# The second transposed m of a Newton iteration, moved from TensorE to a trip through DRAM

## The chip, the cores and the metric

The kernel runs on one NeuronCore of a Trainium2 chip. What counts is the device time of one execution in microseconds (us). Beside it there is a profile of one execution: every instruction of every engine with its start and duration, the packets of the DMA engines, and the semaphores. The engines are called PE (TensorE), DVE (VectorE), ACT (ScalarE), POOL (GpSimd) and SP (SyncE, which here only issues DMAs).

## What is computed

The input x has the shape 32 x 32 x 128 x 128 (images, channels, rows, columns). Two layers follow each other. The first adds to x the matrix square root of a normalised x, by five Newton-Schulz steps on every one of the 1024 matrices of 128 x 128. The second is a spectral layer (Fourier transform, 64 x 32 modes multiplied by weights, inverse transform). The change lies in the first.

```python
A2 = A.reshape(b_s * c, n_c, n_c)
normA = jnp.sqrt(jnp.sum(A2 * A2, axis=(1, 2)))
Y = A2 / normA[:, None, None]
Z = I
for _ in range(5):
    T = 0.5 * (3.0 * I - jnp.matmul(Z, Y))
    Y = jnp.matmul(Y, T)
    Z = jnp.matmul(T, Z)
sA = Y * jnp.sqrt(normA)[:, None, None]

x = x + _L0_conv_ref(_gn(x))
x = x + _L1_conv_ref(_gn(x), L1_conv_weights1, L1_conv_weights2)
```

## The kernel before

The kernel does not run the five steps literally. It works with m, a scaled form of the matrix, and with polynomials of m: two steps at a time are one factor q of degree four, so that the five steps become a first q, a second q, and a last factor t.

**The unit of work** is a set: four channels of one image, held as a tile of 128 x 512 numbers in single precision. There are 256 sets. `products` (L304) multiplies four pairs of 128 x 128 matrices on TensorE into one PSUM bank; `taken` (L271) copies a bank to SBUF on ACT with a factor; `plus` (L279) does bank times factor plus a tile on DVE; `plus_eye` (L290) adds a multiple of the unit matrix on POOL.

TensorE computes the transpose of its left operand times the right one, so a product with m on the left needs m transposed as the left operand. Hence each set carries m and mb, its transposed copy with another scale. Transposes appear in two ways:

- `transposed` (L310) is four TensorE transposes into a bank.
- In `quartic` (L364), the sets called far are turned by way of DRAM: DVE transposes the 32 x 32 blocks (L373), SP writes the result to a DRAM tile (L375), and after some rounds SP reads it back with the blocks in their new places (L383 or L386). POOL then adds r (L388). Sets that are not far use `transposed` and DVE instead. The second `quartic` of a set uses the form called wide, which reads back with four DMAs of 32 partitions each; the first uses one DMA for all 128.

**`newton`** (L400) is the whole course of one set: q from m, mb and r; y from q and m; m from q and y; mb by transposing the new m on TensorE; r from mb; the second q; then two products with that q, the last factor t, and the final product, which DVE adds to xt. It is a generator. Each `yield from rest` gives up the turn twice, and `newton` of a far set gives it up 27 times.

**The order of the work** comes from the loop at the end of the kernel (L997). It has nine lanes, each with one set under way. One pass over all lanes is a round: every lane advances its set by one turn, and between lanes the loop steps other generators: `staged` (normalising the next set, L333), `prep` (statistics of the next image, L187), `settle` and `forward` (what follows a finished set, L426 and L443), `spectrum`, and the products and inverse transforms of the second layer. New sets start at most every FAR = 27/9 = 3 rounds for far sets and every NEAR = 25/5 rounds for others, of which at most about five are under way. A set is far when its image is 1 to 18 (`is_far`, L316, FIRST = 19). So 18 x 8 = 144 sets are far; while they run, little of the second layer's later work is there. I call this time the first stage. The scheduler of the language places instructions by this order and by its own estimate of when they can run; those wrapped in `kept`, all DMAs among them, stay in program order.

**DMA queues.** SP issues writes and reads of the turn buffer, the store of xt to `mid`, and the second layer's transfers. ACT issues the loads b, xt and xs, between its other work.

**Buffers.** `rooms` (L259) gives two numbers for each kind of tile: buffers that exist throughout, and more that exist only until the first stage is over (`four`, L263).

Of the kernel before, what the change touches and what calls it, by code (L numbers as in the profile page):

```python
# [29 lines left out]
F32 = mybir.dt.float32  # L30
AF = mybir.ActivationFunctionType
ALU = mybir.AluOpType
# [4 lines left out]
P = 128  # L37
# [8 lines left out]
QA = 3 + 12 ** (1 / 3)  # L46
QR = 2 * QA - 9
QD = 39 / QA
EYE = 36 / 16
QS = EYE / QD  # L50
MS = -QA * QS
# [17 lines left out]
def conv_preact_kernel(  # L69
# [8 lines left out]
    nc = tc.nc  # L78

    const = ctx.enter_context(tc.tile_pool(name="const", bufs=1))  # L80
    dram = ctx.enter_context(tc.tile_pool(name="dram", bufs=1, space=DRAM))
# [65 lines left out]
    def bank():  # L147
        return ps8.tile([P, 4, P], F32, tag="ps", name="ps")
# [36 lines left out]
    kept = tc.keep_in_program_order  # L185

    def prep(b, made):  # L187
# [12 lines left out]
        for i in range(C // 4):  # L200
# [37 lines left out]
        nc.vector.tensor_scalar_mul(  # L238
            nn, n.rearrange("p g c -> p (g c)"), P * (1.5 / EYE) ** 2
        )  # L240
# [17 lines left out]

    rooms = dict(b=(4, 2), xt=(10, 4), x=(3, 2), r=(5, 2), v=(3, 3), w=(3, 2), q=(4, 2), y=(4, 2))  # L259
    rooms.update(m=(4, 2), mb=(2, 1), t=(3, 2), y4=(2, 2), turn=(0, 4))  # L260
    turns = dict.fromkeys(rooms, 0)

    def four(tag, more):  # L263
        n, m = rooms[tag]
        if more:
            turns[tag] += 1
            if turns[tag] % (n + m) >= n:
                return early.tile([P, 4, P], F32, tag=tag + "_early", name=tag, bufs=m)
        return sets.tile([P, 4, P], F32, tag=tag, name=tag, bufs=n)

    def taken(ps, tag, more, f=1.0):  # L271
        t = four(tag, more)
        if f == 1.0:
            nc.scalar.copy(t, ps)
        else:
            nc.scalar.mul(t, ps, f)  # L276
        return t

    def plus(ps, f, t, tag, more):  # L279

        s = four(tag, more)
        nc.vector.scalar_tensor_tensor(s, ps, f, t, ALU.mult, ALU.add)  # L282
        return s

    def blocks(t):


        return t.rearrange("p c x -> p (c x)").rearrange("p (a c j) -> p a c j", a=4, c=4)

    def plus_eye(mb, far, more):  # L290

        r = four("r", more)
        if far:
            nc.gpsimd.tensor_tensor(
                blocks(r).rearrange("p a c j -> p c a j"),
                mb.rearrange("p c (a j) -> p c a j", a=4),
                eye.rearrange("p c (a j) -> p c a j", a=4),
                ALU.add,
            )
        else:  # L300
            nc.gpsimd.tensor_tensor(r, mb, eye, ALU.add)  # L301
        return r

    def products(lhsT, rhs):  # L304
        ps = bank()
        for j in range(4):
            nc.tensor.matmul(ps[:, j, :], lhsT[:, j], rhs[:, j], start=True, stop=True)  # L307
        return ps

    def transposed(t):  # L310
        ps = bank()
        for j in range(4):
            nc.tensor.transpose(ps[:, j, :], t[:, j, :], ident)
        return ps

    def is_far(b):  # L316
        return 0 < b < FIRST
# [43 lines left out]
        ready.append((xt, m, mb, plus_eye(mb, is_far(b), has_more(b, g))))  # L361
        yield

    def quartic(m, mb, r, far, more, wide):  # L364


        v = plus(products(mb, m), -1 / (QA * QR * QS), m, "v", more)
        if far:


            t = four("turn", more)
            form = "p c (b i) -> p b c i" if wide else "p c (i b) -> p b c i"
            nc.vector.transpose(blocks(t), v.rearrange(form, b=4))  # L373
            held = dram.tile([P, 512], F32, name="turn", tag="turn", bufs=8)
            kept(nc.sync.dma_start(out=held, in_=t.rearrange("p c x -> p (c x)")))  # L375
            yield from rest
            w = four("w", more)
            wb = blocks(w).rearrange("p a c j -> p a (c j)")
            if wide:
                for b in range(4):  # L380
                    rows = slice(32 * b, 32 * b + 32)
                    src = held[:, P * b : P * b + P].rearrange("(a i) x -> i a x", a=4)
                    kept(nc.sync.dma_start(out=wb[rows], in_=src))  # L383
            else:
                src = held.rearrange("(a i) (b x) -> (i b) a x", a=4, b=4)
                kept(nc.sync.dma_start(out=wb, in_=src))  # L386
            yield from rest
            nc.gpsimd.tensor_tensor(w, w, r, ALU.add)  # L388
            w = blocks(w).rearrange("p a c j -> p c a j")
        else:  # L390
            yield from rest
            w = plus(transposed(v), 1.0, r, "w", more)
        yield from rest
        q = plus(products(v, w), 1 / (16 * QS * QS), eye, "q", more)
        yield from rest
        return q

    rest = (None, None)

    def newton(g, sn, xt, m, mb, r, far, more):  # L400


        q = yield from quartic(m, mb, r, far, more, False)
        y = taken(products(q, m), "y", more, 1 / MS)
        yield from rest
        m = taken(products(q, y), "m", more, MS)
        yield from rest
        mb = taken(transposed(m), "mb", more, QR * QS / MS)
        r = plus_eye(mb, far, more)
        yield from rest  # L410
        q = yield from quartic(m, mb, r, far, more, True)
        pw, py = products(q, m), products(q, y)
        w, y = taken(pw, "t", more, 1 / MS), four("y4", more)
        for j in range(4):
            c = 4 * g + j
            nc.scalar.mul(y[:, j, :], py[:, j, :], sn[:, c : c + 1])  # L416
        yield from rest
        t = plus(products(w, q), -0.5 * EYE / 1.5, eye, "t", more)
        yield from rest
        nc.vector.tensor_tensor(xt, products(t, y), xt, ALU.add)  # L420
        yield
# [575 lines left out]
    while todo or any(lanes) or posts or specs or prods or backs:  # L997
# [3 lines left out]
        for i in range(LANES):  # L1001
            step(norms)
            step(loads)
            far = todo and is_far(todo[0][0])
            under_way = [is_far(lane[0]) for lane in lanes if lane]
            room = far or under_way.count(False) + 0.6 * under_way.count(True) < LESS
            if lanes[i] is None and todo and room and rounds >= due:
                due = max(due, rounds - 1) + (FAR if far else NEAR)
                while norms:
                    step(norms)  # L1010
                b, g = todo.pop(0)
                xt = ready[0][0]
# [87 lines left out]
```

## Time and profile before

| What | us |
|---|---|
| median of three runs | 3109.61 |
| lowest and highest run | 3102.69, 3109.81 |
| the profiled execution, its own time | 3100.66 |
| span of the profile, first to last instruction | 3098.6 |
| PE busy in the span | 2948.7 (95%) |
| DVE busy | 2340.0 (76%) |
| POOL busy | 1998.0 (64%) |
| ACT busy | 1704.0 (55%) |
| DMA, mean over the span | 206 GB/s |

The far sets' adds on POOL (L388) start from 108.4 to 1611.8 us, which marks the first stage. Shares over the whole span mix it with the second layer, so the stage has to be read by itself. A product in single precision is two TensorE instructions, a transpose is one; a count of matmuls has to be read with that in mind. Durations of single matmuls overlap, so their price is taken from start to start.

### The profile page before, as it was taken

Reading aid. Unit: us, or ns where it says so; the run is one execution under the profiler, and the core shown is the slowest. Engines: PE = TensorE matmul, PEld = TensorE weight load, DVE = VectorE, ACT = ScalarE, POOL = GpSimd, SP = SyncE. Lnnn points to the kernel's source line nnn. Section 1 sums busy time; section 2 is a strip of 40 time slices with the busy share of each in tenths; the row PEclk is TensorE's granted clock in tenths of the full one; section 3 lists DMA queues with packets and bytes.
Section 4 is the critical chain, followed back from the end, with each engine's and each line's share of the span. In section 5 each row is a group of like instructions: output and inputs, shape, how many; then the busy total and the mean of one; then the engine's idle time right before and its main releaser. Section 6 shows DMA issues by size and latency. Waiting matters only on the chain. (4 is left out here: it accounts for less than half of the span.)

```text
span 3098.6 us, 79471 instructions
## 1 busy us (share of the span) xinstructions
PE 2948.7 (95%) x29760; PEld 2828.6 (91%) x29760; DVE 2340.0 (76%) x5178; ACT 1704.0 (55%) x4153; POOL 1998.0 (64%) x2312
## 2 busy tenths in 40 slices
PE   6999999999999999999999999999999998999994
PEld 6899999999999999999999998998899988899983
DVE  6788887888888787788877555788778766878654
ACT  3566556666665665666654444555454544555552
POOL 3567677677776666677665434768677764777453
PEclk9999999999999999999999999999999999999996
DMA  4576676666666666676743466667676876766666
GB/s 130 164 216 207 202 217 211 210 213 214 212 209 208 209 207 183 201 212 208 219 146 100 143 217 214 226 228 235 206 250 209 269 233 211 236 208 204 194 218 221
DMA packets 475150, 636.78 MB, mean 206 GB/s; under 512 B 97040, under 2 KB 255248, under 8 KB 474768
## 3 DMA queue, kind: packets, MB, share of 16 engines
q1 hardware_dynamic: 361872, 425.88, 42.8%
q10 hardware_dynamic: 112896, 205.83, 21.7%
q8 instruction: 237, 3.88, 0.5%
q14 instruction: 145, 1.19, 0.1%
HBM read 402.42 MB, written 229.11 MB: 204 GB/s over the span
## 5 line engine op out<-in xcount | busy, mean ns | idle before, releaser
L388 POOL TENSOR_TENSOR w<-w,r 128x512 f32<-128x512 f32 x288 | 366.3, 1276 | 324.3 <-DMA w<-turn 274.8
L307 PE MATMUL ps<-w,v 128*128 128x128 f32 x4096 | 554.6, 279 | 18.0 <-DVE w L282 7.7
L341 ACT ACTIVATE b<-b,a_off,a_scr 128x128 f32<-128x128 f32 x1024 | 468.7, 490 | 154.6 <-issue 48.1
L307 PE MATMUL ps<-y,q 128*128 128x128 f32 x4096 | 527.0, 277 | 6.2 <-ACT d L893 2.1
L307 PEld LDWEIGHTS ps<-w,v 128*128 128x128 f32 x4096 | 504.0, 194 | 25.1 <-POOL w L388 11.0
L307 PEld LDWEIGHTS ps<-y,q 128*128 128x128 f32 x4096 | 490.5, 193 | 9.6 <-issue 2.6
L433 POOL TENSOR_TENSOR fold<-xt 128x256 f32<-128x256 f32 x512 | 363.8, 731 | 204.5 <-DVE xt L420 192.2
L282 DVE SCALAR_TENSOR_TENSOR q<-ps,eye 128x512 f32<-128x512 f32 x512 | 348.0, 680 | 156.8 <-PE ps L307 151.5
L827 POOL TENSOR_TENSOR yt<-yt,d 128x512 f32<-128x512 f32 x248 | 311.2, 1282 | 153.7 <-ACT d L893 116.0
L301 POOL TENSOR_TENSOR r<-mb,eye 128x512 f32<-128x512 f32 x112 | 142.7, 1274 | 311.3 <-ACT mb L276 298.8
L348 POOL TENSOR_SCALAR x<-xt,a_nm,a_sc 128x128 f32<-128x128 f32 x736 | 322.7, 451 | 19.5 <-DVE a_n L231 19.5
L416 ACT ACTIVATE y<-ps,a_t_s 128x128 f32<-128x128 f32 x1024 | 291.4, 367 | 58.1 <-PE ps L307 57.6
L202 DVE BATCH_NORM_STATS2 a_st<-xs 128x6 f32<-128x128 f32 x1024 | 229.2, 278 | 108.7 <-DMA xs<-in_xt 107.9
L307 PE MATMUL ps<-m,q 128*128 128x128 f32 x2048 | 276.4, 278 | 8.1 <-DVE q L282 5.2
L307 PE MATMUL ps<-x,b 128*128 128x128 f32 x2048 | 277.0, 279 | 6.8 <-POOL x L348 5.6
L307 PE MATMUL ps<-m,mb 128*128 128x128 f32 x2048 | 276.7, 279 | 6.6 <-ACT d L893 4.3
L307 PE MATMUL ps<-x,q 128*128 128x128 f32 x2048 | 277.8, 279 | 3.3 <-DVE q L282 1.6
L307 PE MATMUL ps<-y,t 128*128 128x128 f32 x2048 | 275.1, 277 | 2.1 <-DVE t L282 2.0
L276 ACT ACTIVATE t<-ps 128x512 f32<-128x512 f32 x256 | 152.3, 595 | 223.1 <-PE ps L307 214.4
L307 PE MATMUL ps<-q,t 128*128 128x128 f32 x2048 | 274.9, 278 | 0.0
L373 DVE STREAM_TRANSPOSE turn<-v 128x512 f32<-128x512 f32 x288 | 262.0, 910 | 4.6
L307 PEld LDWEIGHTS ps<-m,q 128*128 128x128 f32 x2048 | 251.6, 193 | 10.7 <-DVE q L282 5.8
(148 smaller groups left out, 5768.2 us busy)
## 6 DMA issues: line engine op xcount, KB each, us to landing
turn<-turn SPq DMA_DIRECT2D x288, 256.0 KB
b<-in_x ACTq DMA_DIRECT2D x256, 256.0 KB
xt<-in_xt ACTq DMA_DIRECT2D x256, 256.0 KB
xs<-in_xt ACTq DMA_DIRECT2D x256, 256.0 KB
mid<-xt SPq DMA_DIRECT2D x256, 256.0 KB
yt<-mid SPq DMA_DIRECT2D x128, 512.0 KB
out<-yt SPq DMA_DIRECT2D x120, 512.0 KB
w<-turn SPq DMA_DIRECT2D x144, 256.0 KB
```

What stands on the lines that cost most here:

```text
L202: nc.vector.bn_stats(st[:, 4 * i + c, :], tiles[i][:, c, :])
L276: nc.scalar.mul(t, ps, f)
L282: nc.vector.scalar_tensor_tensor(s, ps, f, t, ALU.mult, ALU.add)
L301: nc.gpsimd.tensor_tensor(r, mb, eye, ALU.add)
L307: nc.tensor.matmul(ps[:, j, :], lhsT[:, j], rhs[:, j], start=True, stop=True)
L341: nc.scalar.activation(t, x, AF.Identity, bias=offset[:, c], scale=scale[:, c])
L348: nc.gpsimd.tensor_scalar(m[:, j, :], xt[:, j, :], nm[:, c // 2 : c // 2 + 1], sc[:, c : c + 1], ALU.add, ALU.mult,)
L373: nc.vector.transpose(blocks(t), v.rearrange(form, b=4))
L388: nc.gpsimd.tensor_tensor(w, w, r, ALU.add)
L416: nc.scalar.mul(y[:, j, :], py[:, j, :], sn[:, c : c + 1])
L433: nc.gpsimd.tensor_tensor(f[:, :, 64 * half : 64 * half + 64], xt[:, :, 0:64], xt[:, :, 64:128], op)
L827: engine.tensor_tensor(yh, yh, d, op)
```

## The change

For far sets (`TURNED = 1` takes every one of them), the transposed copy of the second m is made in the way in which v was: block transposes on DVE, a write to DRAM, and reads back. The code of that way becomes a function, `turned`, which always uses the wide form with its four reads. The first `quartic` uses it too. Because mt comes back as m transposed itself, and not as its scaled copy in a bank, the second factor is built the other way round: `quartic` takes m as left and mt as right operand, and mt as what is added. As mt is seen in blocks, the DVE operation for that v is written as four instructions of 128 x 128. In place of the two products of q with m and y, the set computes q times mt, then q times that to form t, then q times t, scaled by ACT, and at last that with y. r is now made from a second copy of the bank that holds m. The buffers change with it: mt gets five, the turn buffer five instead of four, twelve DRAM tiles instead of eight, two more each for y (eight in all), one more each for r and v; b loses one and m two. FAR stays at 27/9, while a far set now gives up its turn 29 times.

```diff
+    rooms.update(mt=(0, 5), turn=(0, 5), b=(4, 1), m=(4, 0), y=(4, 4), r=(5, 3), v=(3, 4), w=(3, 2))
...
-    def quartic(m, mb, r, far, more, wide):
-        v = plus(products(mb, m), -1 / (QA * QR * QS), m, "v", more)
+    def turned(v, tag, more):
+        t = four("turn", more)
+        nc.vector.transpose(blocks(t), v.rearrange("p c (b i) -> p b c i", b=4))
+        held = dram.tile([P, 512], F32, name="turn", tag="turn", bufs=12)
+        kept(nc.sync.dma_start(out=held, in_=t.rearrange("p c x -> p (c x)")))
+        yield from rest
+        w = four(tag, more)
+        wb = blocks(w).rearrange("p a c j -> p a (c j)")
+        for b in range(4):
+            rows = slice(32 * b, 32 * b + 32)
+            src = held[:, P * b : P * b + P].rearrange("(a i) x -> i a x", a=4)
+            kept(nc.sync.dma_start(out=wb[rows], in_=src))
+        yield from rest
+        return w
+
+    def quartic(left, right, f, add, r, far, more):
+        ps = products(left, right)
+        v = four("v", more)
+        whole = len(add.shape) == 3
+        for c in [slice(0, 4)] if whole else range(4):
+            nc.vector.scalar_tensor_tensor(
+                v[:, c] if whole else v[:, c].rearrange("p (a j) -> p a j", a=4),
+                ps[:, c] if whole else ps[:, c].rearrange("p (a j) -> p a j", a=4), f, add[:, c], ALU.mult, ALU.add
+            )
         if far:
...
+            w = yield from turned(v, "w", more)
             nc.gpsimd.tensor_tensor(w, w, r, ALU.add)
...
+    def scaled(ps, g, sn, tag, more):
+        y = four(tag, more)
+        for j in range(4):
+            c = 4 * g + j
+            nc.scalar.mul(y[:, j, :], ps[:, j, :], sn[:, c : c + 1])
+        return y
...
-        m = taken(products(q, y), "m", more, MS)
-        yield from rest
-        mb = taken(transposed(m), "mb", more, QR * QS / MS)
-        r = plus_eye(mb, far, more)
-        yield from rest
-        q = yield from quartic(m, mb, r, far, more, True)
-        pw, py = products(q, m), products(q, y)
-        w, y = taken(pw, "t", more, 1 / MS), four("y4", more)
...
+        pm = products(q, y)
+        m = taken(pm, "m", more, MS)
+        if far and g % TURNED == 0:
+            r = plus_eye(taken(pm, "mb", more, QR * QS), far, more)
+            mt = yield from turned(m, "mt", more)
+            mt = blocks(mt).rearrange("p a c j -> p c a j")
+            q = yield from quartic(m, mt, 1 / (QA * QA * QS), mt, r, far, more)
+            w = taken(products(q, mt), "t", more, 1 / MS)
+            yield from rest
+            t = plus(products(q, w), -0.5 * EYE / 1.5, eye, "t", more)
+            yield from rest
+            t = scaled(products(q, t), g, sn, "y4", more)
+        else:
```

After this, all sets end as before with the product of t and y, which DVE adds to xt. Sets that are not far keep the old course in the branch `else`.

More of the change, by code (lines that the diff above doesn't have):

```diff
@@ L48 @@
 QD = 39 / QA
+TURNED = 1
 EYE = 36 / 16
@@ L362, in staged @@
         yield
-    def quartic(m, mb, r, far, more, wide):
-        v = plus(products(mb, m), -1 / (QA * QR * QS), m, "v", more)
-        if far:
[L371 to L375, printed above, removed]
-            yield from rest
[L377 to L386, printed above, removed]
-            yield from rest
+    def turned(v, tag, more):
[21 more added lines that the diff above has]
+            )
+        if far:
+            w = yield from turned(v, "w", more)
             nc.gpsimd.tensor_tensor(w, w, r, ALU.add)
@@ L398, in conv_preact_kernel @@
     rest = (None, None)
+    def scaled(ps, g, sn, tag, more):
[4 more added lines that the diff above has]
+        return y
     def newton(g, sn, xt, m, mb, r, far, more):
-        q = yield from quartic(m, mb, r, far, more, False)
+        fm = -1 / (QA * QR * QS)
+        q = yield from quartic(mb, m, fm, m, r, far, more)
         y = taken(products(q, m), "y", more, 1 / MS)
         yield from rest
-        m = taken(products(q, y), "m", more, MS)
-        yield from rest
-        mb = taken(transposed(m), "mb", more, QR * QS / MS)
-        r = plus_eye(mb, far, more)
-        yield from rest
-        q = yield from quartic(m, mb, r, far, more, True)
-        pw, py = products(q, m), products(q, y)
-        w, y = taken(pw, "t", more, 1 / MS), four("y4", more)
[L414 to L418, printed above, removed]
+        pm = products(q, y)
[11 more added lines that the diff above has]
+        else:
+            yield from rest
+            mb = taken(transposed(m), "mb", more, QR * QS / MS)
+            r = plus_eye(mb, far, more)
+            yield from rest
+            q = yield from quartic(mb, m, fm, m, r, far, more)
+            pw, py = products(q, m), products(q, y)
+            w = taken(pw, "t", more, 1 / MS)
+            y = scaled(py, g, sn, "y4", more)
+            yield from rest
+            t = plus(products(w, q), -0.5 * EYE / 1.5, eye, "t", more)
         yield from rest
```

## The prediction

> **What bounds the kernel now.** I first asked for the busy time of every engine in a stretch of the first stage (300 to 1300 us), where the change acts.
>
> ```profile
> core 0: us, PE busy (x) PEld busy (x) DVE busy (x) ACT busy (x) POOL busy (x), PEclk, DMA share, GB/s
> 300.00:1300.00 1000.00, 986.59 (x8862) 958.14 (x8861) 818.98 (x1831) 605.12 (x1497) 698.20 (x772) 0.99 0.68 207
> ```
>
> The groups of this stretch count 193 block transposes, two a set, so 96.5 sets pass in 1000 us: 10.36 us a set. TensorE is the bound: busy 98.7% at a granted clock of 0.99, and in the groups by shape hardly any matmul idles before it starts. The reader should note what stands second and third: DVE 82%, the 16 DMA engines 68%. The timeline of TensorE then gives the price of what is removed.
>
> ```profile
> 604.65 0.63 PE L313 MATMUL ps<-ident,z 128*128 128x128 f32 x4
> 605.12 0.60 PE L313 MATMUL ps<-ident,m 128*128 128x128 f32 x4
> 605.56 1.06 PE L307 MATMUL ps<-w,v 128*128 128x128 f32 x8
> 606.45 0.72 PE L307 MATMUL ps<-x,b 128*128 128x128 f32 x5
> ```
>
> Start to start, four transposes take 605.56 - 605.12 = 0.44 us, and the eight matmuls of one product of four 606.45 - 605.56 = 0.89 us. Third, the DVE timeline: the two block transposes of a set are not alike.
>
> ```profile
> 610.62 1.13 DVE L373 STREAM_TRANSPOSE turn<-v 128x512 f32<-128x512 f32 x1
> 611.65 0.68 DVE L420 TENSOR_TENSOR xt<-ps,xt 128x512 f32<-128x512 f32 x1
> ...
> 614.35 0.71 DVE L373 STREAM_TRANSPOSE turn<-v 128x512 f32<-128x512 f32 x1
> ```
>
> The one after the first v (form "i b", strided by four elements) takes 1.13, that of the second (form "b i") 0.71. Fourth, the DMA view and the timeline of SP's queue.
>
> ```profile
> q1 hardware_dynamic: 173189, 130.02, 41.7%
> q10 hardware_dynamic: 41502, 75.56, 25.3%
> ...
> turn<-turn SPq DMA_DIRECT2D x193, 256.0 KB
> ...
> w<-turn SPq DMA_DIRECT2D x97, 256.0 KB
> w<-turn SPq DMA_DIRECT2D x387, 64.0 KB
> ...
> 630.21 0.32 SPq L375 DMA_DIRECT2D turn<-turn  x1
> 631.03 1.77 SPq L383 DMA_DIRECT2D w<-turn  x4
> ```
>
> SP's q1 takes 41.7% of the engines, ACT's q10 25.3%. A "b i" turn is one write and four reads of 64 KB, which hold SP 1.77 us; an "i b" turn needs one read. Last, the waits.
>
> ```profile
> POOL w L388 <- DMA w<-turn: 196.2, 77, 8.3
> ACT mb L276 <- DMA w<-turn: 4.6, 2, 2.4
> SPq L375 <- DMA w<-turn: 16.3, 12, 3.7
> ```
>
> POOL waits for turned tiles in 77 of 193 cases: the round trip through DRAM is already only just in time. The other two name DMAs whose data the waiter does not read. The trace's semaphores explain them: all 2749 DMAs that SP and ACT issue share eight completion semaphores in turn, so the ninth waits until the first has landed, and ACT's evacuations stand behind ACT's issues.
>
> **What the skill says.** The Trainium skill, "DMA: Bandwidth & Descriptors", section "Issuing engines are not separate DMA queues": SP's and ACT's DMAs interleave on the same 16 engines. The trace agrees: 41.7% and 25.3% add up to the 68%. Its section "Two DMAs through the same engine are not ordered" says a DMA that reads what another wrote must be issued after a wait on the first one's semaphore. SP's queue does wait so (L383 on turn<-turn, 18 times, 21.2 us here). "Perfetto Trace Analysis", section "Per-instruction lifecycle", says an issue's reported time ends before the data has moved; I therefore take landings from the semaphores' last increments. "VectorE: DVE Perf Modes", on the TRN2 errata: each instruction pays a fixed extra. Here bn_stats over 128 elements takes 277 ns, over 256 419: 1.1 ns an element and 135 fixed.
>
> **The change part by part**, for one of the 144 sets of the first stage (18 images of 8 sets).
>
> TensorE loses the four transposes of m, 0.44 us. Products stay ten: q·m and q·y on one side, against q·mt and q·(t) on the other. Floor: 10.36 - 0.44 = 9.92 us.
>
> ACT: m, mb, y, t and four scaled copies before and after; mb now leaves from the same bank as m. Nothing, and POOL's three adds stay too.
>
> DVE: turns were 1.13 + 0.71, and are 3 x 0.71, so +0.29. The second v is no longer one 677 ns instruction but four of 128 elements, since mt is seen in blocks. Nearest row, bn_stats at 128 elements: 4 x 277 - 677 = +0.43. Bounds: +0.1, if their ends overlap, and +0.6. Sum 8.49 + 0.72 = 9.2 us, 93% of 9.92. It stays below TensorE, but queues longer.
>
> SP: before, writes 2 x 0.33, a wide read 4 x 0.46, a narrow one 0.50, the store of xt 0.58 (means of this stretch): 3.6 us. After, 3 x 0.33 + 12 x 0.46 + 0.58 = 7.1 us of 9.92, with the semaphore waits between them not counted. All that follows stands behind it in order: the stores of xt, the spectra, and every later turn.
>
> DMA engines: 0.676 x 10.36 = 7.0 us a set. A third turn adds 128 packets of 2 KB at 91 ns and 512 of 512 B at 28.8 ns over 16 engines, 0.73 + 0.92, and 8 more DMAs' completion packets 0.07: 8.7 us, 88% of 9.92. In 5 us stretches the packets' share tops out near 1.0 at about 300 GB/s, so there is room, but little.
>
> Completion semaphores: landing takes 3.04 us on average for a wide read, 3.25 for a write to the turn buffer, 4.65 narrow read, 4.16 xt store, 3.9 to 4.6 ACT's loads. Today 11.1 DMAs a set occupy the eight slots 49%. After: 12 + 3 + 1 + 3 + 0.1 = 19.1 DMAs. At unchanged landing times 12 x 3.04 + 3 x 3.25 + 4.16 + 12.9 + 0.5 = 63.8 us of slot time, 8.0 us a set, 80% of 9.92. But landing times grow with load: over 5 us stretches with a share near 0.66 the mean DMA takes 3.2 us, near 0.80 3.7, near 0.86 4.8, above 0.9 5.1. This mix is lighter (3.34 against 3.67 at the mean load, factor 0.91). At a period of 9.92 us: share 0.88, 4.4 us x 19.1 / 8 = 10.5 us of slots, more than there is. At 10.4: 9.8 us, 94%. At 10.9: about 8.5 us, 78%. Issue in order cannot fill slots to 94%; today, at 49%, a tenth of the DMAs already find theirs just freed.
>
> Latency of mt: this is new on the path. From the end of the product for m to the product m·mt lie four rounds of the lane loop. The lane's 27 waits become 29; a lane is refilled after one more round, so a set takes 30/9 = 3.33 rounds instead of 28/9. At 9.92 us a round is 2.98 us, and four less the product itself 11.0 us. Needed, with today's means: ACT starts m 1.44 after the product, 0.60 for it, DVE's queue about 0.9, turn 0.71, write 3.25, four issues 1.35, landing 3.04, some 0.2 of hand-overs: 11.5 us. Unlike w, which has POOL and two more rounds as cushion (PE takes w 3.8 us, median, after POOL ends), mt has TensorE itself waiting, with all products queued behind it. At 10.85 us four rounds give 12.1.
>
> Buffers: the additions fit y's, r's and mt's longer lives; m goes from six to four and b from six to five. m lives some five rounds, under two sets: nothing. b: from nothing to a few us.
>
> I take 10.85 us, between the two slot figures and where mt's 11.5 plus half a us of extra queueing fits: +0.49 x 144 = +71 us. On the execution's own 3100.7 us (span 3098.6) this is 3171; the median of the runs is 9 above that execution, so I say 3175.
>
> **Rivals.** (1) TensorE stays the bound: if the semaphores never hold SP for long and the scheduler places other sets' products in front of m·mt, the whole 0.44 x 144 = 63 us goes, 3037 to, with some of it lost, 3085. For it: TensorE is nearly gapless today and every other engine's sum stays below 9.92. Against: 19.1 DMAs over eight slots. It decides if the mean landing stays under 9.92 x 8 / 19.1 = 4.15 us. (2) Slots and savings cancel: period 10.3 to 10.45, within 0.3%, about 3105. (3) mt's latency dominates: write and reads each a microsecond slower and SP a microsecond behind at both gives some 14 us, so (14 + 0.9) / 4 = 3.7 us a round and 12.4 a set; less what longer rounds give back, 11.5 to 12 us a set, 3265 to 3340. For it: SP at 70%; against: longer rounds relieve the DMAs. That the transposes are not removed can be excluded: the branch calls none, and only the 112 other sets keep theirs.
>
> **Numbers.** Forecast (slower, 3120 to 3230) 0.46; rival 1 0.20; rival 2 0.12; rival 3 0.22. The range 3065 to 3300 cuts off the best part of rival 1 and the worst of rival 3, under 2 in 10; the forecast's own is 3120 to 3230. A difference under 0.3%, some 9 us, can't be told from none. Faster 0.20, same 0.12, slower 0.68.
>
> **What would show it.** ident,m falls from 1024 to 448 matmuls, DVE's turns all take 0.71, and SP's issues roughly double. If I am right, PE busy in this stretch falls to about 92%, with idle ended by DMA mt<-turn or by w, SP and ACT wait for DMAs they don't read, and the sets' period is near 10.85. I am wrong if PE stays above 98% and the period falls to 10.0, or if DVE ends the waits. The second stage should not change.

## The result and the profile after

The changed kernel takes 3550.28 us in the median (four runs, 3541.08 to 3562.79), the kernel before 3108.94 beside it: a ratio of 1.1427, interval 1.1385 to 1.1469. The forecast was 3175, in a range of 3065 to 3300. The sign was right, the size not: +71 us were forecast, +441 came.

The page of the changed kernel, as far as it answers to the lines shown of before: busy time, two rows of the 40 slices, the DMA queue of SP, and its issues.

```profile
PE 3039.1 (86%) x29184; PEld 2895.1 (82%) x29184; DVE 2413.2 (68%) x5754; ACT 1703.0 (48%) x4153; POOL 2000.5 (56%) x2312
...
PE   7888887788887788878788999999999999998995
...
PEclk9898989998999899998999999999999999999996
...
q1 hardware_dynamic: 472464, 501.45, 45.4%
...
turn<-turn SPq DMA_DIRECT2D x432, 256.0 KB
```

TensorE idles from the first slices to about the 22nd and is full after that: the time is lost in the first stage, where the change acts. The POOL adds of the far sets now run over 1904 us from first to last, before over 1503: +401. What follows the last of them takes 45 us more than before, the first comes 1 us sooner, and the spans, 3542.8 against 3098.6, differ by 444. The stretch of 300 to 1300 us, with the columns as in the prediction:

```profile
300.00:1300.00 1000.00, 821.46 (x6741) 788.05 (x6742) 682.25 (x1758) 478.08 (x1187) 552.69 (x610) 0.92 0.69 203
```

TensorE went from 98.7% to 82%, its granted clock from 0.99 to 0.92, and the DMA share from 0.68 only to 0.69: the engines do no more in a microsecond than before. Where TensorE idles is told by the groups by shape and the waits, here of 400 to 1400 us:

```profile
L309 PE MATMUL ps<-mt,m 128*128 128x128 f32 x616 | 109.0, 332 | 177.1 <-DMA mt<-turn 109.3 <-DMA w<-turn 54.1 <-DVE q L284 4.4
L370 DVE STREAM_TRANSPOSE turn<-v 128x512 f32<-128x512 f32 x153 | 108.0, 706 | 3.2
```

The 153 turns of v, two a set, say 76.5 sets, so 13.07 us a set instead of 10.36. Of 183 us in which TensorE is idle, 177.1 stand before one product, the one of mt and m (the view names a read of w as its second releaser; followed set by set, the product starts 0.24 us after its own mt has landed, on average). What such a wait does is seen in TensorE's timeline:

```profile
807.68 1.06 PE L309 MATMUL ps<-w,v 128*128 128x128 f32 x8
814.25 2.05 PE L309 MATMUL ps<-mt,m 128*128 128x128 f32 x8 [5.50 <-DMA w<-turn]
816.09 1.92 PE L309 MATMUL ps<-x,b 128*128 128x128 f32 x8
817.79 1.62 PE L309 MATMUL ps<-t,q 128*128 128x128 f32 x8
819.25 0.60 PE L315 MATMUL ps<-ident,sw 128*128 128x128 f32 x4
819.68 1.06 PE L309 MATMUL ps<-w,v 128*128 128x128 f32 x8
```

After 5.50 us without work a product takes 2.05 us instead of 1.06, and the next two start 1.84 and 1.70 after the one ahead of them, not 0.89. The three together last 819.25 - 814.25 = 5.0 us, 2.3 more than three at full rate. So this wait is paid for nearly one and a half times. The Trainium skill, "TensorE: Matmul & The Clock Gate", section "What's actually happening", says that after an idle window of about 3.4 us the array falls to half rate until it has been busy for as long; this trace agrees in kind, with some 5 us of slow products. So a set's 13.07 us are 2.39 of idle time (183 / 76.5) and 10.68 of work, of which 0.76 above the 9.92 that the prediction gave the ten products at full clock.

And why mt is late is seen in SP's queue. At 805.53 it starts to issue the four reads of mt that the product at 814.25 waits for:

```profile
805.09 0.34 SPq L372 DMA_DIRECT2D turn<-turn  x1
805.53 6.42 SPq L379 DMA_DIRECT2D mt<-turn  x4
812.06 3.81 SPq L379 DMA_DIRECT2D w<-turn  x8
```

Four reads take 1.8 us to issue where nothing holds them (four reads of w at 802.41); here they take 6.42, so that the last leaves at 811.95, 2.3 us before the product starts. SP's waits, 400 to 1400 us:

```profile
SPq L372 <- DVE turn L370: 197.5, 98, 4.8
SPq L379 <- DMA b<-in_x: 35.7, 25, 2.5
SPq L379 <- DMA w<-turn: 29.9, 28, 2.3
SPq L379 <- DMA xs<-in_xt: 21.4, 19, 3.5
```

SP issues in order. A write that waits for its transpose on DVE (197.5 us) holds up every read behind it; a read (L379) waits for b or xs, loads that ACT issued and that a read of mt has nothing to do with, because all DMAs of SP and ACT take eight completion semaphores in turn. I call such a semaphore a slot. Followed through the records of 400 to 1400 us, each write paired with the read that stands behind it in the program, mt's trip has these means, from the start of ACT's copy of m to the product:

| step | us | in the prediction |
|---|---|---|
| ACT copies m | 0.60 | 0.60 |
| until DVE starts | 0.64 | 0.9 |
| block transpose | 0.70 | 0.71 |
| until SP issues the write | 1.52 | none |
| write lands | 3.01 | 3.25 |
| until SP issues the first read | 3.62 | none |
| first to last read issued | 2.27 | 1.35 |
| last read lands | 2.86 | 3.04 |
| until the product starts | 0.24 | 0.2 |
| sum | 15.45 | 10.05 |

The prediction's 11.5 us also has the time from the end of the product for m to ACT's copy, 1.44 us, which came out at 0.40. The parts are those of a kernel that has already slowed: at 13.07 us a set a round takes 13.07 x 9 / 30 = 3.92 us, four of them 15.7. As the reads stand two rounds behind the write in SP's order, longer rounds also move the reads back. How much of the 3.62 us is cause and how much follows from the longer rounds is not separated by any run.

### The profile page after: what moved, and what is told of

Read it like the earlier page. It is cut to its first block, busy times and chain, and to the rows that moved or that the text cites. A ratio compares the mean times of both kernels' runs of the same rounds, so it can differ in the third digit from the quotient of the medians.

```text
span 3542.8 us, 80917 instructions
## 1 busy us (share of the span) xinstructions
PE 3039.1 (86%) x29184; PEld 2895.1 (82%) x29184; DVE 2413.2 (68%) x5754; ACT 1703.0 (48%) x4153; POOL 2000.5 (56%) x2312
## 5 line engine op out<-in xcount | busy, mean ns | idle before, releaser
L309 PE MATMUL ps<-mt,m 128*128 128x128 f32 x1152 | 203.2, 332 | 336.8 <-DMA mt<-turn 202.1
L309 PEld LDWEIGHTS ps<-mt,m 128*128 128x128 f32 x1152 | 176.0, 234 | 356.3 <-issue 308.9
L309 PE MATMUL ps<-y,q 128*128 128x128 f32 x2944 | 390.9, 279 | 20.3 <-ACT d L922 14.2
L309 PEld LDWEIGHTS ps<-y,q 128*128 128x128 f32 x2944 | 359.7, 194 | 24.2 <-ACT d L922 15.0
L278 ACT ACTIVATE y<-ps 128x512 f32<-128x512 f32 x256 | 152.3, 595 | 395.4 <-PE ps L309 392.4
L309 PE MATMUL ps<-t,q 128*128 128x128 f32 x2304 | 325.7, 287 | 1.9 <-DVE t L284 1.9
L309 PE MATMUL ps<-x,q 128*128 128x128 f32 x2048 | 304.6, 297 | 7.2 <-DVE q L284 5.6
L309 PEld LDWEIGHTS ps<-t,q 128*128 128x128 f32 x2304 | 300.5, 204 | 4.7 <-DVE t L284 2.7
L278 ACT ACTIVATE m<-ps 128x512 f32<-128x512 f32 x256 | 154.1, 602 | 299.3 <-PE ps L309 293.8
L309 PEld LDWEIGHTS ps<-x,q 128*128 128x128 f32 x2048 | 280.2, 212 | 9.2 <-DVE q L284 6.2
```

## The experiments

Each kernel is compared with the kernel before on the same chip. "First stage" is the time from the first to the last of the far sets' POOL adds in its profile (before: 1503 us). "SP held by ACT" is worked out from the semaphores' records of 400 to 1400 us: time in which SP waited for a completion semaphore whose last user was a load issued by ACT. A turn is wide when it is read back with four DMAs, narrow when with one.

| kernel | median, us | ratio, interval | first stage | SP held by ACT |
|---|---|---|---|---|
| the change | 3550.28 | 1.1427 (1.1385 to 1.1469) | 1904 | 103 |
| e1_unused | 3812.47 | 1.2283 (1.223 to 1.2337) | 2155 | 390 |
| e2_no_trip | 3194.09 | 1.0291 (1.0261 to 1.0321) | 1550 | 51 |
| e3_half | 3386.33 | 1.091 (1.0879 to 1.0942) | 1739 | 77 |
| e4_soon | 3676.97 | 1.1847 (1.1759 to 1.1934) | 2040 | 225 |
| e6_narrow | 3407.77 | 1.0968 (1.0936 to 1.1) | 1761 | 0 |
| b1_wide | 3103.64 | 0.9999 (0.9985 to 1.0014) | 1505 | 20 |
| b2_rooms | 3109.83 | 1.0008 (0.9997 to 1.0018) | 1497 | 3 |
| b3_rests | 3159.94 | 1.017 (1.0141 to 1.02) | 1511 | 0 |
| f1_nar_unused | 3191.49 | 1.0288 (1.0236 to 1.0341) | 1545 | 2 |
| f2_nar_later_l10 | 3233.87 | 1.0425 (1.0379 to 1.0471) | 1582 | 0 |
| f3_nar_l10 | 3348.33 | 1.0794 (1.0759 to 1.0829) | 1710 | 0 |
| f4_nar_no_trip | 3126.78 | 1.0087 (1.004 to 1.0134) | 1476 | 0 |
| g1_unused_sp | 3760.76 | 1.2105 (1.2019 to 1.2191) | 2143 | 0 |
| g2_wide_later_l10 | 3766.04 | 1.2122 (1.204 to 1.2203) | 2112 | 371 |
| g3_mixed | 3296.99 | 1.0612 (1.0539 to 1.0685) | 1668 | 8 |
| g4_mixed_half | 3232.72 | 1.0405 (1.0334 to 1.0476) | 1581 | 7 |
| h1_unused_pool | 3680.29 | 1.1838 (1.1802 to 1.1874) | 2026 | 367 |
| h2_wide_kept | 3651.93 | 1.1747 (1.172 to 1.1773) | 1994 | 337 |

In e1, e2, f1, f4, g1 and h1, m itself stands where mt belongs: these kernels leave out the use of the transpose, and their products are the same in number and shape.

### The parts of the change

**e1_unused** makes the trip and uses m in its place; **e2_no_trip** leaves the trip out and keeps the rests.

```diff
-            mt = yield from turned(m, "mt", more)
-            mt = blocks(mt).rearrange("p a c j -> p c a j")
+            yield from turned(m, "mt", more)           # e1; in e2: yield from rest, twice
+            mt = m.rearrange("p c (a j) -> p c a j", a=4)
```

> The trip of the second m through DRAM is made in full (DVE turn, write, four reads), but the products take m itself where they took mt, so the second factor of the far sets is computed from the wrong operand and nothing waits for mt. Same number of rounds, DMAs and products. Theory W (TensorE waits for mt: the trip takes 15.5 us and four rounds do not cover it): the waits go, about 10.0 to 10.3 us a set, 3040 to 3090 us. Theory S (the load of 19 DMAs a set on eight completion semaphores and SP's queue): the load is all there, so it stays above 3200 us.

> As the run before, but the trip of m is left out (no turn, no write, no reads), two rests in its place; again the products use m for mt. Theory W: no more than 30 us below the run with the unused trip, about 3040 us. Theory S: this one reaches about 3040 us and the one with the unused trip does not.

Without the trip the first stage is 1550 us, 354 shorter than the change's: nearly all of the loss comes with the trip. But with the trip made and nobody waiting for it, the kernel is slower still, 2155. Theory S had only said that e1 stays above 3200 us; that it would be slower than the change was forecast by no theory, and neither was e2's 3194. So in the wide form the trip can cost in a second way, besides TensorE's wait for its data. The waits of e1, of TensorE, POOL and SP in 400 to 1400 us:

```profile
PE ps L309 <- POOL w L397: 216.3, 75, 6.4
```

```profile
POOL r L296 <- ACT b L343: 173.4, 32, 10.6
POOL fold L462 <- DVE xt L449: 145.5, 34, 9.3
POOL r L296 <- ACT mb L278: 138.3, 28, 8.1
POOL w L397 <- DMA w<-turn: 20.5, 11, 5.3
```

```profile
SPq L379 <- DMA b<-in_x: 193.5, 36, 14.3
SPq L372 <- DMA b<-in_x: 68.6, 13, 9.4
SPq L379 <- DMA xs<-in_xt: 67.7, 32, 8.5
SPq L372 <- DVE turn L370: 42.2, 26, 7.2
```

TensorE hardly waits for DMA data any more (25 us in all); it waits for POOL's w, which stands behind an r that waits for ACT. SP almost never waits for work (42.2 us for DVE's turns): it issues for 470 us and is held for 390 by slots of ACT's loads. One such hold, in the timelines of SP and of ACT:

```profile
1289.67 1.74 SPq L379 DMA_DIRECT2D w<-turn  x4
1300.87 0.34 SPq L372 DMA_DIRECT2D turn<-turn  x1
```

```profile
1295.71 0.60 ACT L278 ACTIVATE y<-ps 128x512 f32<-128x512 f32 x1 [7.25 <-PE ps L309]
1297.76 0.37 ACT L561 COPY z<-ps 128x256 f32<-128x256 f32 x1 [1.45 <-PE ps L552]
1297.82 0.33 ACTq L329 DMA_DIRECT2D b<-in_x  x1
```

SP is free at 1291.41 and issues nothing until 1300.87. The semaphore that its write is to use belongs, in the program's order, to a load of b. ACT has not even issued that load: it stands behind a copy of y that waits 7.25 us for TensorE. It goes out at 1297.82 and lands at 1300.81, and SP follows. Of e1's 390 us, 160 pass before ACT has issued the load.

One thing limits what e1 says. Its edit takes away a dependence, and the scheduler then lays another order. Over the first stage TensorE runs the same sequence of matmuls in the change, e1, e6 and f1, but of POOL's instructions 80% stand in another place in e1 than in the change, 18% by more than two places. So e1 is the change without the wait and with another order on POOL. In the narrow form the same edit moves little: 6% between e6 and f1, none by more than two places.

**e3_half** takes the trip for every second set only (`TURNED = 2`). **e4_soon** puts both rests behind the reads of mt, so that these follow their write at once:

```diff
-        yield from rest
+        if tag == "w":
+            yield from rest
         w = four(tag, more)
...
         yield from rest
+        if tag == "mt":
+            yield from rest
```

> Every second far set takes the new way, the others the old. Theory W: TensorE still stalls for each turned set, 72 of 144; the loss of 441 us at least halves, 3150 to 3330 us. Theory S: 15 DMAs a set fit the slots easily (some 60%), nothing is lost and half the transposes are saved, about 3075 us.

> For mt alone the four reads are issued right behind the write, without the two turns between, and both rests come after them; the number of rounds stays. In the changed kernel the reads began 4.1 us after the write had landed, so theory W expects a trip shorter by some 3 to 4 us and a time of 3150 to 3350 us, with SP itself standing about 2.5 us a set for the landing. Theory S expects 3500 us or more, since the same DMAs pass and SP stands longer.

Half the trips leave the first stage at 1739, close to the middle between e2's 1550 and the change's 1904 (1727): the cost goes with the number of trips. The 3386 us of e3 lie above what either theory gave. The earlier reads make it worse (2040), as theory S had it:

```profile
PE ps L309 <- POOL w L400: 150.4, 69, 5.6
PE ps L309 <- DMA mt<-turn: 20.9, 12, 3.7
```

```profile
SPq L380 <- DMA turn<-turn: 171.5, 87, 4.5
```

The reads stand in SP's queue and wait for their write to land, and all behind them wait too. mt itself now lands 2.4 us before its product (mean), and TensorE waits little for it; instead it waits for POOL's w as in e1. The place of the reads is not simply chosen too late. The same shows in every wide kernel made from the change: TensorE's longest wait is for POOL's w, from 48.9 us in 1000 without the trip (e2) and 59.5 with half the trips (e3) to 233.1 (g1). In the narrow ones it is 24.8 at most (f1), in the change 2.0.

**e6_narrow** makes all three turns narrow: one read of 256 KB in place of four, and the strided transposes of the old first turn.

```diff
-        nc.vector.transpose(blocks(t), v.rearrange("p c (b i) -> p b c i", b=4))
+        nc.vector.transpose(blocks(t), v.rearrange("p c (i b) -> p b c i", b=4))
...
-        for b in range(4):
-            rows = slice(32 * b, 32 * b + 32)
-            src = held[:, P * b : P * b + P].rearrange("(a i) x -> i a x", a=4)
-            kept(nc.sync.dma_start(out=wb[rows], in_=src))
+        src = held.rearrange("(a i) (b x) -> (i b) a x", a=4, b=4)
+        kept(nc.sync.dma_start(out=wb, in_=src))
```

> The changed kernel with the other form of turn in all three places: one read of 256 KB for all 128 partitions in place of four of 64 KB, and DVE's strided transpose of 1.13 us in place of 0.71. DMAs a set fall from 19 to 10. Theory S (the number of DMAs, which share eight completion semaphores between SP and ACT, so that SP's queue stands for loads that ACT has not issued yet): most of the loss goes, 3060 to 3180 us. Theory R (29 waits instead of 27 on nine lanes leave less work in a round to cover the trips): above 3300 us, as the trips and rounds are the same.

142 us come back in the median and 143 in the first stage, although DVE pays 1.11 instead of 0.70 for every turn. Theory S had expected most of the loss to go (3060 to 3180); 3408 is in theory R's range. TensorE and SP in 400 to 1400 us:

```profile
PE ps L309 <- DMA mt<-turn: 123.1, 58, 6.2
```

```profile
SPq L372 <- DVE turn L370: 513.7, 190, 10.5
SPq L377 <- DMA turn<-turn: 51.2, 48, 3.1
```

SP now waits for work half of the time, and no load of ACT holds it. Yet TensorE still waits for mt: the trip is 14.09 us long, with 2.56 between landing and read, and a landing of 4.69 for the one large read.

### Before with one part of the change

**b1_wide** makes the first turn of before wide too (`quartic(m, mb, r, far, more, True)`); **b2_rooms** gives before the change's buffers (the new `rooms.update` without mt); **b3_rests** gives its far sets one more rest ahead of the end, so that they give up their turn 29 times as in the change:

```diff
         t = plus(products(w, q), -0.5 * EYE / 1.5, eye, "t", more)
         yield from rest
+        if far:
+            yield from rest
         nc.vector.tensor_tensor(xt, products(t, y), xt, ALU.add)
```

> The kernel before with one thing of the change: the first turn of a far set reads back in four DMAs as the second does. 14 DMAs a set instead of 11, DVE 0.4 us a set less; rounds and buffers as before. Theory S: it loses what the run without the trip lost, 3150 to 3200 us. Theory R and theory B (fewer buffers for m and b): no loss, 3095 to 3110 us.

> The kernel before with the change's numbers of buffers alone (m four instead of six, b five instead of six, more of y, r, v and turn). Theory B: 3130 to 3200 us. Theories S and R: 3095 to 3115 us.

> The kernel before with one more rest before the last product of a far set, so that it gives up its turn 29 times as in the change; the same work, DMAs and buffers. Theory R: 3130 to 3200 us. Theories S and B: 3095 to 3115 us.

In the kernel before, two wide turns a set cost nothing that can be measured, nor do the buffers. Neither carries over to the change as it stands: there y and r live longer in their buffers and mt is new, b2 leaves the DRAM tiles at eight, and without mt's trip two wide turns do cost against two narrow ones (a first stage of 1550 in e2, 1476 in f4 below). The 29 turns cost some 54 us, but nearly all behind the first stage (1511): after it b3 needs 1453 us from the last far set to the last set, before 1399, the change 1442, e2 without a trip also 1442. So the 43 us that the change needs more there go with the longer course of the far sets, not with the trip. How it delays what follows was not looked into.

### The narrow form taken apart

**f1_nar_unused** is e6 with m in mt's place, trip made; **f4_nar_no_trip** is e6 without the trip; **f3_nar_l10** is e6 with ten lanes (`LANES, LESS = 10, 5`); **f2_nar_later_l10** is f3 with one rest more between the reads of mt and its use.

> Both at once: every turn reads back in one DMA, and the trip of m is made but m is used where mt was, so its result is not waited for and the second factor of the far sets is computed from the wrong operand. Theory S (shared completion semaphores tie SP's queue to ACT's): with 10 DMAs a set nothing ties them, and without the wait TensorE runs near its floor, 3050 to 3130 us. Theory W+S (the wait for mt costs what the narrow form left over): the same. If the order of the instructions on the engines is the cause, it stays above 3250 us.

> The trip of m left out (the products use m itself, so the second factor of the far sets is computed from the wrong operand), and the other two turns in the narrow form: 8 DMAs a set. With the wide form this was 3194 us. Theory S: the rest of its loss in the first stage was the 14 DMAs, so 3070 to 3110 us. If it was the order or the rounds: 3180 to 3200 us.

> Narrow turns everywhere and ten lanes, no further rest. The rounds per set fall from 3.33 to 3.0 and get longer, so four of them cover 13.2 us at 9.9 us a set. Theory W+S: between the narrow run with nine lanes (3408 us) and the one with the further rest, 3200 to 3350 us. If the number of sets under way were the limit: 3050 to 3150 us already here.

> Narrow turns everywhere, one more rest between mt's read and its use, and ten lanes instead of nine, so that a set still starts about every 3.2 rounds; it computes the whole result. Theory W+S: mt's trip of some 14 us now has six rounds, 19 us, and is covered: 3050 to 3150 us. If the waits for mt only move elsewhere: 3350 us or more.

Only f3 is inside a forecast range, at its edge. f1, f2 and f4 lie between theirs: f1 midway, f2 somewhat nearer to theory W+S, f4 nearer to theory S. The first stages fit a latency: without the trip 1476; made but unused 1545; used 1761; used, but with six rounds and ten lanes, 1582. TensorE's waits in f2 no longer name mt at all. What is left is 67 us in 1000 (before: 11), in many small waits, of which these are the largest:

```profile
PE ps L309 <- DVE q L284: 14.7, 8, 2.9
PE ps L309 <- POOL w L397: 9.9, 11, 2.0
PE ps L309 <- ACT y L413: 9.8, 3, 3.8
```

mt has then landed 5.35 us before its product starts (mean), and the gap from landing to the read is 0.80. The tenth lane alone gives 51 us of the first stage (f3), the further `yield from rest` with it another 128. Every one of these kernels stays slower than before: with no wait for mt, f2 still needs 79 us more than before's first stage and some 50 after it.

### What the wide form loses beyond the wait

If waiting for mt were all, e1 should have come near f1. It was 610 us of first stage above it. **g1_unused_sp** is e1 with the loads of b, xt and xs issued by SP (`nc.scalar.dma_start` becomes `nc.sync.dma_start` at L195, L329 and L330), so that no slot is shared between two queues. **g2_wide_later_l10** is the change with f2's extra rest and ten lanes.

> The run with the wide trip whose result is unused (3812 us), with the loads b, xt and xs issued from SP instead of ACT, so that the completion semaphores are no longer shared between two queues; the same 19 DMAs a set, 8.3 us of issue on SP; the second factor of the far sets again takes m for mt. Theory S (SP stood for loads which ACT, itself standing behind TensorE's products, had not issued yet): 3150 to 3450 us. If the number of issues on SP is the cause: no gain, 3800 us or more.

> The change as it is (wide turns), with the further rest before the use of mt and ten lanes, which brought the narrow form from 3408 to 3234 us. If the wait for mt and the tie of the two queues add up, the tie's part stays: 3400 to 3650 us. If six rounds hide the tie as well: 3230 to 3300 us.

Neither helps: 2143, 12 us less than e1, and 2112, more than the change. Both medians lie outside the ranges given. In g1 no load of ACT can hold SP, and yet TensorE waits for POOL's w as in e1 (233.1 us). Its waits, of POOL and SP:

```profile
POOL r L296 <- ACT b L343: 216.8, 38, 11.6
POOL r L296 <- ACT mb L278: 155.6, 35, 9.1
```

```profile
SPq L372 <- DVE turn L370: 257.6, 76, 9.3
```

So the shared slots by themselves are not the cause, striking as they are in e1's trace. What remains in view is a loop of engines that each work in order: TensorE waits for POOL's w, w stands behind r, r waits for ACT's b or mb, and ACT stands behind copies that wait for TensorE (y in g1: 224.6 us). The scheduler lays this order. I counted POOL's adds in 400 to 1400 us: at each w, how many sets' r(b) have gone ahead, less half of the w's so far, as a set has two. The mean is 4.33 sets in e1 and 4.47 in g1, but 3.51 in e6 and f1 and 3.68 in the kernel before: w is laid relatively later. **h1_unused_pool** and **h2_wide_kept** test that: h1 is e1 with POOL's r and w kept in the program's order, h2 is g2 with all instructions of the sets on TensorE, DVE, ACT and POOL kept so.

```diff
-            nc.gpsimd.tensor_tensor(w, w, r, ALU.add)
+            kept(nc.gpsimd.tensor_tensor(w, w, r, ALU.add))
```

> As e1 (mt's trip made, m used in its place, 3812 us), but POOL's two adds, r and w, keep the order in which the program states them. As in e1, m is used in place of mt, so the second factor is not the reference's. Theory O (the instructions of the engines are laid in an order in which POOL's w stands behind an r that waits for ACT, and TensorE's next product behind that w): POOL's adds come off that loop, far fewer waits of TensorE on POOL (now 474 us in 1000), 3200 to 3500 us. Theory R2 (the order on POOL is only where the lateness shows, its cause lies on another engine): 3750 us or more.

> As g2 (wide turns, mt used one rest later, ten lanes, 3766 us), but every instruction of the sets on TensorE, DVE, ACT and POOL keeps the order of the program. Theory O (the loss of the wide form beyond mt's trip comes from the order in which the scheduler lays the instructions): 3150 to 3350 us, near the narrow form's 3234. If the number of DMAs or the landing of their data costs the time whatever the order: 3650 us or more. Between the two: order is a part of it.

h1 fell between the theories. h2, at 3652, is at the edge of the range given for the rival, that the number of DMAs or their landing costs the time whatever the order. h1 lost 129 of the 610 us that e1's first stage stands above f1's, h2 118 of the 530 that g2's stands above f2's. What was changed of the order is worth about a fifth. The lag of w behind r fell to 3.79 sets in h1, the change's own value (3.78), and h1 is still slower than the change; in h2 it fell only from 4.60 to 4.32 (f2: 3.81). So the program's own order keeps much of the lag, h2 tests the theory less sharply than it was meant to, and the lag by itself doesn't give the time. In h1 POOL's r waits far less for ACT, but TensorE's wait for w only falls from 216.3 to 192.3, and POOL then stands before fold:

```profile
POOL fold L462 <- DVE xt L449: 273.7, 49, 10.8
POOL w L397 <- DMA w<-turn: 62.9, 25, 5.3
POOL r L296 <- ACT mb L278: 62.8, 15, 7.8
```

And in h2, with every engine in the program's order, SP is filled again:

```profile
SPq L379 <- DMA b<-in_x: 106.7, 35, 7.9
SPq L372 <- DMA b<-in_x: 78.2, 16, 11.6
...
SPq L372 <- DVE turn L370: 17.4, 12, 5.2
```

It issues for 526 us, is held by ACT's slots for 337, and waits 17.4 for DVE. g1 took away the shared slots, h1 and h2 changed the order; both together were not tried. How one tie stands in for the other can be read from w's way, in means of 400 to 1400 us:

| kernel | v's block transpose to w's landing | w's landing to POOL's add |
|---|---|---|
| f1 | 9.7 | 0.6 |
| the change | 12.0 | 1.0 |
| e1 | 16.8 | 4.7 |
| g1 | 11.9 | 9.3 |
| h1 | 16.3 | 3.2 |
| h2 | 16.4 | 3.6 |

Without shared slots w lands 4.9 us sooner (g1 against e1), and POOL takes it 4.6 us later; the sum stays near 21 us. The two that mix the forms, **g3_mixed** (mt and the first v narrow, the second v wide, f2's extra rest and ten lanes, the last two rests one turn each) and **g4_mixed_half** (the same with `TURNED = 2`), were built to beat before:

> A version meant to be good: ten lanes, the further rest for mt, the last two rests of a set shortened to one turn each (29 turns), narrow turns for mt and the first v, the wide one for the second v (13 DMAs a set, DVE 0.4 us less than all narrow). It computes the whole result. Both mechanisms small: 3080 to 3200 us; DVE's relief and fewer rounds should bring it below the 3234 us of the narrow one.

> As the run before it, but only every second far set turns m through DRAM. Half the saving (32 us at the floor), DVE and DMAs between the old and the new way: 3060 to 3150 us.

They don't, and both missed their ranges. In g3 TensorE waits for DVE's last factor t, 59.6 us in 1000, which suggests that the shortened rests came too close. g4 and f2 are the fastest kernels that use mt's trip, g4 for half of the sets, and both are 4% slower than before. No version was found that beats it.

## Why the prediction was wrong

**The bound, the removed transposes and the engines' sums** held. `ident,m` fell to 448 matmuls, all turns take 0.70 to 0.71, SP issues for 537 / 76.5 = 7.0 us a set (7.1 forecast), DVE is at 8.9 us a set (9.2 forecast; the v in four parts costs 0.88 instead of 0.68, so +0.20 and not the +0.43 taken, inside the bounds). Of the 63 us that the transposes seemed worth, f4, the kernel without mt's trip, shows 27 in the first stage. Of the prediction's own signs, TensorE's idle time does end with the landing of mt, but TensorE is busy 82% and not 92%.

**The step that failed is "Latency of mt"**. Its sum of 11.5 us took each part at its mean and gave SP's queue nothing: a write was to be issued when its data was there, and the reads as soon as it had landed. The runs showed 1.52 us ahead of the write, 3.62 between landing and first read, and 2.27 in place of 1.35 for the reads: 6.1 us, more than the whole miss of 4.4 (15.45 and 0.40 against 11.5), since ACT began sooner and the landings came out a little shorter. The prediction had 7.1 us of issues on SP and "All that follows stands behind it in order" in one paragraph, and did not carry this into the sum further on. That such a wait costs the time is shown for the narrow form: using mt instead of m costs 216 us (f1 to e6), and with two rounds more and a tenth lane TensorE's wait for mt is gone and 179 us of the first stage with it (f2), 51 of them by the lane alone (f3). In the wide form of the change the trip as a whole costs 354 us (e2), and how these divide between this wait and the ties of POOL and SP stays open.

**"Completion semaphores" mis-sized the other way.** It took landing times to grow with load until slots were the limit, at 10.85 us a set. All DMAs landed in 3.30 us on average (before 3.67), the DMA share was 0.69, the slots were occupied 60% of the time. What the traces show in its place is a matter of order: a slot is handed on in the program's order between two queues, so that SP waits for a load that has just been issued (103 us in 1000 in the change), or, in kernels like e1, has not been issued yet. The prediction saw such waits in the trace of before and priced them as an occupancy. Its test for rival 1, a mean landing under 4.15 us, came true without rival 1: the slots had room, and mt was late all the same.

**Rival 3 was nearest**: it named mt's latency, TensorE waiting and SP behind at write and reads, but at a microsecond each, hence 11.5 to 12 us a set and at most 3340. Its sum also slips: 11.5 and four times a microsecond are 15.5, not 14, and (15.5 + 0.9) / 4 x 30 / 9 is 13.7 us a set before any relief, near the 13.07 measured, not 12.4. The relief that it expected from longer rounds did not come, since SP's queue keeps its order and stretches with them. It also left out what an idle TensorE costs afterwards: 0.76 us a set at the lower clock, some 110 us over 144 sets. (A smaller slip: 3171 and 9 are 3180, not 3175.)

**"The second stage should not change"** was wrong by 43 us, and b3 shows that the 29 turns suffice for them.

The ledger of the first stage, by way of the narrow form, in us:

| from, to | first stage | difference |
|---|---|---|
| before | 1503 | |
| transposes gone, no trip, narrow (f4) | 1476 | -27 |
| trip made, not used (f1) | 1545 | +69 |
| trip used (e6) | 1761 | +216 |
| wide in place of narrow: the change | 1904 | +143 |

The rows +69 and +216 are shown by runs that differ in that point and little in the scheduler's order (POOL 14% and 6% of the places, DVE 28% and 16%, most of them by one or two). The first row is the difference of two kernels that differ in more: far sets with 29 turns, other buffers, the second factor built the other way. The last is open in its mechanism: the scheduler's order differs too (46% of POOL's places). In the kernel before it is neither the buffers (b2) nor wide turns (b1); in kernels with the trip it is not ACT's slots alone (g1), and what h1 changed of POOL's order is a fifth of the 610 us between e1 and f1. Without the trip the wide form already costs 74 us (e2 against f4). Where the wide trip is not waited for (e1) or is given more time (g2), the loss is even larger, which a longer latency can't explain. My reading is that with twelve reads a set SP's queue has no slack left, and that any lateness then comes back to it through ACT's loads or through POOL's order, so that one tie stands in when the other is cut. The table of w's way fits this. It is argued from the traces, not shown.

## What to carry to other kernels

When a value leaves for a trip through a queue that issues in order, add the queue's own waits at each of its steps, ahead of the write, between landing and read, and over the issues: here they were 6 of 15 us, and the landings did not grow at all. Two queues that shared completion semaphores held each other up here as one queue would, when an engine issued loads between its other work; taking that away alone gave 12 us (g1). TensorE's stalls cost more than themselves here, 0.76 us of slow products on 2.39 us of idle time a set. And when an experiment removes a wait, look whether the scheduler has laid another order too (e1).

## What the runs showed that was not expected

- A kernel that makes a trip and ignores its result was 262 us slower than the one that waits for it (e1 against the change), with POOL's instructions in another order.
- SP stood idle up to 14.3 us for a load of another queue, for 11.3 of them before that load was issued, though the two share no data (e1).
- One large read lands later than the last of four small ones, 4.69 against 2.86 us, and was still the choice of the faster kernel (e6); that this is for its one issue and one slot was not shown apart.
- DVE's block transpose with a stride of four elements takes 1.11 us, without it 0.70; in b1 this gain of 0.4 us a set changed nothing that can be measured.
